# Turning the first experts' rows two blocks ahead, and loading their weights one round sooner

## The chip, the cores and the metric

The kernel runs on one core of a Trainium2 chip. The metric is the device time of one execution in microseconds, as the median of several runs. All engines of the core have their own instruction queues: PE (TensorE), DVE (VectorE), ACT (ScalarE), POOL (GpSimd) and SP (SyncE, which here only issues transfers). An engine works through its queue in order and waits on semaphores that other engines or transfers raise.

## The reference

Two layers follow one another on 32 sequences of 56 tokens with 256 features. What matters here is the first mixture of experts: 16 experts of width 176, six chosen for each token.

```python
x = x + _L0_xattn_ref(_layernorm(x), ctx_2048, ...)   # a scan over 1500 context rows, only its mean is used
x = x + _L0_ffn_ref(_layernorm(x), ...)               # 16 experts, width 176, top 6
x = x + _L1_xattn_ref(_layernorm(x), ctx_2048, mask)  # masked attention over the context
x = x + _L1_ffn_ref(_layernorm(x), ...)               # 2 experts, width 1024, top 1

# _L0_ffn_ref, for the tokens h
scores = softmax(h @ gate_w.T)
topk_w, topk_idx = top_k(scores, 6)
for e in range(16):
    out = silu(h @ w_gate[e].T) * (h @ w_up[e].T) @ w_down[e].T
    y = y + cw[:, e:e+1] * out                        # cw: the chosen scores, zero elsewhere
```

## The kernel before

The kernel has four stages in time. The context stage reads the whole context (32 loads of 1.5 MB into a ring of five slots), makes the first layer's sum, normalizes the tokens, and sorts the tokens by expert. The first experts' stage runs over 95 blocks of 128 sorted rows. Then come the second layer's attention and its two experts.

**The context stage** goes in rounds. A round `p` (two sequences, 112 tokens) calls the steps of a list in an order written out by hand, each for its own `p` plus an offset. Tokens are written as normalized rows: `second_norm` makes the tile `xn` on ACT (L563), out of a pool of four buffers, so that the tile of one `p` takes the buffer of `p - 4`; `away` (L569) sends it from SP to `xn0` in HBM. In round `p` it is `away(p - 1)` that is issued. `count_in` reads a ring slot on PE (L339) and issues the load of the context five sequences on (L155, SP).

**The first experts' weights** come on the same SP queue. `load_w0_up` issues four transfers of 1.4 MB (L206: 2,048 pieces of 704 bytes each) after round 12, the last of `away(11)`. The down weights are 26 small transfers (L222) of 8 to 88 partitions; `some_pieces(n)` issues the next `n` of them, here six after round 13, six after round 14, and the other 14 in the tail, after `away(b)` and `away(c)`.

**The tail** finishes the last three rounds' tokens, called a, b and c in the code (13, 14 and 15). Its order is also written by hand. It ends with `idx`, the table of the row numbers of all 95 blocks, and `wgt`, their weights (L902, L903). `busy(n)` puts n matmuls on PE whose result nobody reads. The sort of a token group needs `tokens_in` (ACT, L655), `ones_at` or `low_ones` (DVE, L666), `more_ones` (POOL, L674) and `last_ones` (ACT, L692 and L695) before `sorted_low` and `sorted_high` (PE, L702).

**The first experts' stage** is `expert_blocks` with one unit a block. `rows_of` gathers a block's 128 rows from `xn0` into a tile `xb` (POOL, L1092, eight buffers, seven gathers ahead). It reads all of `xn0`, so the first gather waits for every `away` to have landed, and for `idx`. `turned_rows` transposes `xb` on PE and copies it to `xT` on ACT (L191, L193, three buffers). In iteration `t`, PE does: gate and up matmuls of block t (L933), transposes of the hidden rows of block t-1 (L951), transposes of the rows of block t+1 (L191), down matmuls of block t-2 (L960). ACT does: the activation of block t (L939), the copy of `xT` of block t+1 (L193), the copy of the result of block t-2 (L1100). DVE multiplies and copies (L945, L953). Beside these, `side(t)` puts in small work of the next stage; among it up to one or two gathers of finished rows an iteration on POOL (L1007), from iteration 20 on.

Of the kernel before, what the change touches and what calls it, by code (L numbers as in the profile page):

```python
# [22 lines left out]
NP = B // 2  # L23
# [37 lines left out]
def xattn_ffn_kernel(  # L61
# [149 lines left out]
    def w0_down_pieces():  # L211

        half = E0 // 2
        for e in range(half):
            for c in range(2):
                r = 0
                while r < H0:
                    f = e * F0 + c * H0 + r
                    n = min(H0 - r, P - f % P)
                    o = 2 * KD * F0 + c * D  # L220
                    k = f // P
                    yield lambda r=r, n=n, e=e, o=o, f=f, k=k: nc.sync.dma_start(  # L222
                        out=w0_sb[r : r + n, e :: half, o : o + D],
                        in_=wd0[f % P : f % P + n, k :: half * F0 // P, :][:, 0:2, :],
                    )
                    r += n

    with tc.tile_pool(name="p1", bufs=1) as p1, tc.tile_pool(name="p3", bufs=3) as p3, tc.tile_pool(
# [185 lines left out]
        def first_stats(o):  # L414
            for p in range(o, o + 4):
                V.bn_stats(out=st[:, p, :], in_=xr[:, p, :])
                V.bn_aggr(out=mva[:, p, :], in_=st[:, p, :])
            inverse_root(rsa[:, o : o + 4], mva[:, o : o + 4, 1])

        def first_bias(o):  # L420
            q = slice(o, o + 4)
            V.scalar_tensor_tensor(nba[:, q], mva[:, q, 0], -1.0, rsa[:, q], ALU.mult, ALU.mult)
# [145 lines left out]
        def away(p):  # L568
            nc.sync.dma_start(out=xn0[p * P : (p + 1) * P, :], in_=pend[p]["xn"])  # L569
# [23 lines left out]
        def scores_out(p):  # L593
            A.copy(lgs[p % 2][:, 0:E0], pend[p]["lp"][:, 0:E0])
# [58 lines left out]
        def tokens_in(p):  # L653
            v = vals[:, p % 2]
            A.activation(v[:, :, 0, :], v[:, :, 0, :], AF.Copy, scale=ids[:, p : p + 1])  # L655

        def hots(p, h):
            t = pend[p].setdefault("hots", {})
            if h not in t:
                t[h] = ohp.tile([P, NE, P], F32, tag="oh", name="oh")  # L660
            return t[h]

        def ones_at(p, h, n=NE):

            o = NE * h
            V.tensor_tensor(  # L666
                hots(p, h)[:, 0:n], iota.unsqueeze(1).to_broadcast([P, n, P]),
                pend[p]["off"][:, o : o + n].unsqueeze(2).to_broadcast([P, n, P]), ALU.is_equal,
            )
# [9 lines left out]
        def busy(n, w=512):  # L679

            for _ in range(n):
                d = psa.tile([P, 512], F32, tag="acc", name="d")
                PE.matmul(
                    d[:, 0:w], lhsT=ident, rhs=ones[:, 0:1].to_broadcast([P, w]),
                    start=True, stop=True,
                )

        def last_ones(p, h, n):

            t, off = hots(p, h)[:, n:NE], pend[p]["off"]  # L690
            for i in range(n, NE):
                A.activation(  # L692
                    t[:, i - n], iota, AF.Abs, bias=off[:, NE * h + i : NE * h + i + 1], scale=-1.0
                )
            A.activation(t, t, AF.Relu, bias=ones[:, 0:1], scale=-1.0)  # L695
# [19 lines left out]
        def low_ones(p):  # L715
            ones_at(p, 0)
# [16 lines left out]
        pieces = list(w0_down_pieces())  # L733


        def some_pieces(n):
            for _ in range(n):
                if pieces:
                    pieces.pop(0)()
# [22 lines left out]
        for p in range(last):  # L762
            for step, d in steps if p == last - 1 else steps + ends:
                if 0 <= p + d < NP:
                    step(p + d)
            if p < 3:
                first_stats(4 * p + 4)
                first_bias(4 * p + 4)
            if p == NP - 4:
                load_w0_up()  # L770
            if p > NP - 4:
                some_pieces(6)


        at_ = slots[B % NRING].rearrange("p j d -> p (j d)")[0:1, CW - 2 * E0 * NLP :]
        G.memset(at_, 0.0)
        at_ = at_.rearrange("p (e o l) -> p e o l", e=E0, o=2)
        a, b, c = last - 2, last - 1, last
        scores_out(a)
        sum_in_columns(c)  # L780
# [24 lines left out]
        away(b)  # L805
        second_norm(c)
        away(c)
        some_pieces(len(pieces))
        places(a)
        turned(b)  # L810
        more_high_ones(a)
# [22 lines left out]
        PE.matmul(tot[:, 0:E0], lhsT=ones, rhs=chosen[:, b % 2], start=False, stop=True)  # L834
        more_high_ones(b)
        ranks(c)
        busy(2)
        real = p2.tile([P, NL, E0], F32, name="real")
        V.tensor_tensor(
            real, tot[:, 0:E0].unsqueeze(1).to_broadcast([P, NL, E0]), lev, ALU.is_gt  # L840
# [20 lines left out]
        for k in range(4):  # L861
# [3 lines left out]
                rhs=ones[0:1, 0:1], start=True, stop=True,  # L865
            )
        low_ones(c)
        last_ones(c, 1, 6)
        tokens_in(c)
        ones_at(c, 1, 6)  # L870
        sorted_low(c)
        blk = p2.tile([P, 4], F32, name="blk")
# [41 lines left out]
    def expert_blocks(nb, nq, f, w, ei, wk, ptr, pgu, pht, py, rows_of, done, ahead, wgt=None, side=None, xT0=None):  # L914

        fp = f // nq
        h = fp // 2
        doff = 2 * KD * fp
        piece = doff + 2 * D
        units = [(i, u) for i in range(nb) for u in range(nq)]  # L920
        xT, at, hs, hT, y = {}, {}, {}, {}, {}

        def expert_at(i):
            at[i] = PE.value_load(
                ei[0:1, i : i + 1], min_val=0, max_val=w.shape[1] - nq * piece
            )

        def gate_up(i, u):
            if u == 0 and i not in at:
                expert_at(i)  # L930
            gu = pgu.tile([P, 512], F32, tag="gu", name="gu")
            for k in range(KD):
                PE.matmul(  # L933
                    gu[:, 0 : 2 * fp], lhsT=xT[i][:, k, :],
                    rhs=w[:, bass.ds(at[i] + (u * piece + k * 2 * fp), 2 * fp)],
                    start=(k == 0), stop=(k == KD - 1),
                )
            sg = wk.tile([P, fp], F32, tag="sg", name="sg")
            A.activation(sg, gu[:, 0:fp], AF.Silu)  # L939
            hs[i, u] = wk.tile([P, fp], F32, tag="hs", name="hs")  # L940
            up = gu[:, fp : 2 * fp]
            if wgt is None:
                V.tensor_tensor(hs[i, u], sg, up, ALU.mult)  # L943
            else:
                V.scalar_tensor_tensor(hs[i, u], sg, wgt[:, i : i + 1], up, ALU.mult, ALU.mult)  # L945

        def turn(i, u):
            tp = pht.tile([P, 512], F32, tag="ht", name="tp")
            a = hs.pop((i, u))
            for c in range(2):  # L950
                PE.transpose(tp[0:h, c * P : (c + 1) * P], a[:, c * h : (c + 1) * h], ident)  # L951
            hT[i, u] = wk.tile([h, 2 * P], F32, tag="hT", name="hT")
            V.tensor_copy(hT[i, u], tp[0:h, 0 : 2 * P])  # L953

        def down(i, u):
            if u == 0:
                y[i] = py.tile([P, 512], F32, tag="y", name="y")
            a = hT.pop((i, u))
            for c in range(2):
                PE.matmul(  # L960
                    y[i][:, 0:D], lhsT=a[:, c * P : (c + 1) * P],
                    rhs=w[0:h, bass.ds(at[i] + (u * piece + doff + c * D), D)],
                    start=(u == 0 and c == 0), stop=(u == nq - 1 and c == 1),
                )
            if u == nq - 1:
                done(i, y.pop(i))

        xb = {i: rows_of(i) for i in range(min(ahead, nb))}
        if not xT0:
            unread(ptr, "tr", 512, 512, 512, 256)  # L970
            expert_at(0)
        xT[0] = xT0 or turned_rows(wk, ptr, "tr", xb[0])
        xb.pop(0)
        if side:
            side(-1)
        for t in range(len(units) + 2):
            if t < len(units):
                gate_up(*units[t])
            if 0 <= t - 1 < len(units):
                turn(*units[t - 1])  # L980
            if t < len(units) and units[t][1] == nq // 2 and units[t][0] + 1 < nb:
                i = units[t][0] + 1
                if i + ahead - 1 < nb:
                    xb[i + ahead - 1] = rows_of(i + ahead - 1)
                xT[i] = turned_rows(wk, ptr, "tr", xb.pop(i))
            if t >= 2:
                down(*units[t - 2])
            if side:
                side(t)
# [89 lines left out]
    with tc.manual_schedule(  # L1079
# [10 lines left out]
        def rows_of(i):  # L1090
            xb = xbp.tile([P, D], F32, tag="xb", name="xb")
            G.indirect_dma_start(  # L1092
                out=xb, out_offset=None, in_=xn0,
                in_offset=bass.IndirectOffsetOnAxis(ap=idx[:, i : i + 1], axis=0),
            )
            return xb
# [170 lines left out]
    with tc.manual_schedule(  # L1267
# [214 lines left out]
        for p in range(NP + 1):  # L1482
# [17 lines left out]
            if p < NP:  # L1500
                nb = highest(sps)
# [159 lines left out]
    with tc.tile_pool(name="g", bufs=2) as gp, tc.tile_pool(name="g1", bufs=1) as g1, tc.tile_pool(  # L1661
# [12 lines left out]
        for p in range(NP):  # L1674
# [41 lines left out]
            nb = small.tile([P, 3], F32, tag="nb", name="nb")  # L1716
# [119 lines left out]
```

## Time and profile before

| | us |
|---|---|
| median of 3 runs | 703.46 |
| lowest, highest | 700.73, 703.96 |
| the profiled execution's own time | 743.97 |
| its span | 742.3 |
| PE busy | 674.1 (91%) |
| DVE, ACT, POOL busy | 386.9, 258.5, 318.0 |
| HBM traffic | 136.63 MB, 184 GB/s over the span |

The profiled execution took 40.5 us more than the median of the runs. Its durations are those of the instructions and waits in that execution, so a sum of them belongs to 743.97 us first. PE's busy time counts matmuls whose ends are modelled. The page gives shares over the whole span, while the change touches two places: the end of the context stage (about 130 to 186 us) and the first experts' stage (about 186 to 470 us).

### The profile page before, as it was taken

What the parts mean: (1) busy time and instruction counts of PE and PEld (TensorE: products, weight loads), DVE (VectorE), ACT (ScalarE), POOL (GpSimd) and SP (SyncE); (2) the same over time, 40 slices, a digit from 0 to 9 for tenths busy, and PEclk for the clock granted to TensorE, in tenths of its full rate; (3) what the DMA queues carried; (4) which work ended last, traced back from release to release, by engine and by line L of the source; (5) the groups of instructions that cost most, each with busy time, mean ns of one, the idle gap of its engine ahead of it and who ended that gap; (6) DMA issues with size and microseconds to landing.
All of it is one profiled execution on the core that took longest, in us unless ns stands there. A gap on an engine that the chain in (4) does not pass through costs nothing.

```text
span 742.3 us, 13524 instructions
## 1 busy us (share of the span) xinstructions
PE 674.1 (91%) x4111; PEld 434.3 (59%) x4111; DVE 386.9 (52%) x1310; ACT 258.5 (35%) x772; POOL 318.0 (43%) x416
## 2 busy tenths in 40 slices
PE   7789999998799888898898888999897999999997
PEld 3345565654577565566676655566554666666564
DVE  5548888885256344343353436568787332323232
ACT  0224555542244333333343332476552111111110
POOL 3104454544543664667656655558423302122111
PEclk7858999998899999999999999999999999999999
DMA  8999999995489874444444444595941201010100
GB/s 272 337 406 404 410 411 411 384 287 147 133 260 282 292 217 149 121 128 128 135 128 136 128 124 119 149 329 79 333 143 62 88 15 33 32 38 28 35 30 18
DMA packets 71273, 136.63 MB, mean 184 GB/s; under 512 B 8026, under 2 KB 43772, under 8 KB 71196
## 3 DMA queue, kind: packets, MB, share of 16 engines
q1 hardware_dynamic: 56042, 100.31, 38.6%
q0 software_dynamic: 14096, 34.52, 17.1%
q10 hardware_dynamic: 1058, 0.86, 0.4%
q8 instruction: 38, 0.62, 0.4%
q14 instruction: 39, 0.32, 0.1%
HBM read 109.54 MB, written 26.77 MB: 184 GB/s over the span
## 4 chain that ended last, share of the span: by engine, by line
PE 65%; DVE 4%; issue 2%; ACT 2%; SPq 1%; DMA 1%; POOL 0%; another core or an unknown queue 0%; POOLq 0%; ACTq 0%; DVEq 0%
PE gu L933 30%; PE y L960 19%; PE tp L951 4%; PE tp L191 3%; PE tp L1064 3%; PE sp L1294 2%; PE op L1329 2%; SPq L222 1%; ACT xT L193 1%; PE tp L1053 1%; PE tp L1321 1%; PE sp L1288 1%; DMA w_sb<-in_wd 1%; DMA xs<-pay,to 0%; POOL oh L674 0%
## 5 line engine op out<-in xcount | busy, mean ns | idle before, releaser
L933 PE MATMUL gu<-w_sb,xT 128*128 x380 | 134.3, 476 | 29.4 <-ACT xT L193 19.8
L939 ACT ACTIVATE sg<-gu 128x176 f32<-128x176 f32 (+1 forms) x155 | 53.3, 344 | 247.0 <-PE gu L933 213.0
L1092 POOL DMA_INDIRECT xb<-xn,idx x95 | 94.0, 989 | 95.5 <-PE tp L191 43.3
L945 DVE SCALAR_TENSOR_TENSOR hs<-sg,wgt,gu 128x176 f32<-128x176 f32 x95 | 37.7, 397 | 154.5 <-ACT sg L939 129.2
L933 PE MATMUL gu<-ring,xT 128*128 x240 | 113.8, 597 | 0.0
L933 PEld LDWEIGHTS gu<-w_sb,xT 128*128 128x128 f32 x380 | 69.9, 192 | 65.4 <-ACT xT L193 27.8
L960 PE MATMUL y<-w_sb,hT 88*128 x380 | 98.6, 382 | 1.6 <-ACT yb L1100 1.6
L1007 POOL DMA_INDIRECT g<-ys,early x78 | 74.6, 956 | 35.3 <-issue 20.4
L943 DVE TENSOR_TENSOR hs<-sg,gu 128x256 f32<-128x256 f32 x60 | 25.3, 421 | 112.2 <-ACT sg L939 108.3
L951 PEld LDWEIGHTS tp<-ident,hs 128*88 128x88 f32 (+1 forms) x310 | 40.3, 130 | 58.7 <-issue 47.9
L960 PEld LDWEIGHTS y<-w_sb,hT 88*128 88x128 f32 x380 | 65.0, 191 | 7.4 <-ACT yb L1100 2.0
L1580 POOL DMA_INDIRECT out<-ob,ti x15 | 14.8, 990 | 126.9 <-DVE ob L1577 126.6
L674 POOL TENSOR_SCALAR oh<-iota,off 128x128 f32<-128x128 f32 x60 | 42.5, 722 | 59.0 <-PE owned L702 39.8
L953 DVE COPY hT<-tp 88x256 f32<-88x256 f32 (+1 forms) x155 | 64.4, 415 | 4.8 <-PE y L960 4.0
L933 PEld LDWEIGHTS gu<-ring,xT 128*128 128x128 f32 x240 | 45.6, 192 | 33.3 <-issue 30.5
L339 PE MATMUL acc<-ring,cz 128*32 128x256 f32 x768 | 57.0, 438 | 5.8 <-DMA ring<-in_cx 5.4
L960 PE MATMUL y<-ring,hT 128*128 x240 | 61.7, 380 | 0.0
L951 PE MATMUL tp<-ident,hs 128*88 128x128 f32 (+1 forms) x310 | 59.5, 274 | 0.0
L193 ACT COPY xT<-tp 128x256 f32<-128x256 f32 x110 | 41.0, 373 | 41.9 <-PE y L960 21.3
L1100 ACT COPY yb<-y 128x256 f32<-128x256 f32 x95 | 35.7, 376 | 47.0 <-PE y L960 27.2
L191 PE MATMUL tp<-ident,xb 128*128 128x128 f32 x220 | 42.5, 275 | 0.9 <-DMA xb<-xn,idx 0.9
L960 PEld LDWEIGHTS y<-ring,hT 128*128 128x128 f32 x240 | 41.0, 190 | 3.3
(315 smaller groups left out, 967.5 us busy)
## 6 DMA issues: line engine op xcount, KB each, us to landing
ring<-in_cx SPq DMA_DIRECT2D x32, 1536.0 KB
ys<-yb SPq DMA_DIRECT2D x95, 128.0 KB
ring<-in_cx SPq DMA_DIRECT2D x16, 384.0 KB
extra<-in_cx SPq DMA_DIRECT2D x16, 384.0 KB
xs<-zrow SPq DMA_DIRECT2D x5, 771.0 KB
w_sb<-in_wg SPq DMA_DIRECT2D x2, 1408.0 KB
w_sb<-in_wu SPq DMA_DIRECT2D x2, 1408.0 KB
xn<-xn SPq DMA_DIRECT2D x16, 128.0 KB
```

The costliest lines, as they stand in the source:

```text
L191: PE.transpose(tp[:, k * P : (k + 1) * P], xn[:, k * P : (k + 1) * P], ident)
L193: A.copy(xT.rearrange("p k c -> p (k c)"), tp[:, 0 : KD * P])
L339: PE.matmul(acc[Q * g : Q * g + Q, 0:D], lhsT=cz[:, j, 1 - h : 1 - h + Q], rhs=c[:, j, :], start=(h == 0 and m == 0), stop=(h == 1 and m = ...
L674: G.tensor_scalar(hots(p, h)[:, i, :], iota, pend[p]["off"][:, NE * h + i : NE * h + i + 1], None, ALU.is_equal,)
L933: PE.matmul(gu[:, 0 : 2 * fp], lhsT=xT[i][:, k, :], rhs=w[:, bass.ds(at[i] + (u * piece + k * 2 * fp), 2 * fp)], start=(k == 0), stop=(k = ...
L939: A.activation(sg, gu[:, 0:fp], AF.Silu)
L945: V.scalar_tensor_tensor(hs[i, u], sg, wgt[:, i : i + 1], up, ALU.mult, ALU.mult)
L951: PE.transpose(tp[0:h, c * P : (c + 1) * P], a[:, c * h : (c + 1) * h], ident)
L953: V.tensor_copy(hT[i, u], tp[0:h, 0 : 2 * P])
L960: PE.matmul(y[i][:, 0:D], lhsT=a[:, c * P : (c + 1) * P], rhs=w[0:h, bass.ds(at[i] + (u * piece + doff + c * D), D)], start=(u == 0 and c ...
L1007: G.indirect_dma_start(out=g, out_offset=None, in_=ys0[0 : n * P, :], in_offset=bass.IndirectOffsetOnAxis(ap=at[:, p, k : k + 1], axis=0),)
L1092: G.indirect_dma_start(out=xb, out_offset=None, in_=xn0, in_offset=bass.IndirectOffsetOnAxis(ap=idx[:, i : i + 1], axis=0),)
```

## The change

Four edits. The rows of a first-experts block are transposed and copied two blocks before they are used, in place of one (block 1 and block 2 still one ahead; in iteration 2 both block 3 and block 4). The gate and up weights' four transfers are issued after round 11, in place of round 12, and so stand on SP's queue ahead of `away(11)`. The down weights are issued eight after each of the rounds 12, 13 and 14, and the other two at the start of the tail, so that all 26 stand ahead of `away(b)` and `away(c)`, in place of 12. In the tail, one of two unread matmuls is left out of `busy`, and `tokens_in(c)` goes ahead of `last_ones(c)` on ACT. The second experts' blocks, which also use `expert_blocks`, keep their order (`nq > 1`).

```diff
-            if p == NP - 4:
+            if p == NP - 5:
                 load_w0_up()
-            if p > NP - 4:
-                some_pieces(6)
+            if p > NP - 5:
+                some_pieces(8)
...
+        some_pieces(len(pieces))
         a, b, c = last - 2, last - 1, last
         scores_out(a)
...
         away(b)
         second_norm(c)
         away(c)
-        some_pieces(len(pieces))
         places(a)
...
         ranks(c)
-        busy(2)
+        busy(1)
...
         low_ones(c)
+        tokens_in(c)
         last_ones(c, 1, 6)
-        tokens_in(c)
         ones_at(c, 1, 6)
...
+        def turned_at(i, u):
+            if nq > 1:
+                return [j for j in (i + 1,) if u == nq // 2 and j < nb]
+            return [j for j in ((i + 1,) if i < 2 else (3, 4) if i == 2 else (i + 2,)) if j < nb]
...
-            if t < len(units) and units[t][1] == nq // 2 and units[t][0] + 1 < nb:
-                i = units[t][0] + 1
+            for i in turned_at(*units[t]) if t < len(units) else ():
                 if i + ahead - 1 < nb:
                     xb[i + ahead - 1] = rows_of(i + ahead - 1)
                 xT[i] = turned_rows(wk, ptr, "tr", xb.pop(i))
```

## The prediction

> **What bounds the kernel now.** First the times by stage, in four windows cut at the first and the last experts' matmuls (columns: PE, weight loads, DVE, ACT, POOL busy, granted clock, DMA share, GB/s).
>
> ```profile
> 0.00:186.30 186.30, 164.56 (x1694) 95.16 (x1694) 134.19 (x459) 76.96 (x263) 72.64 (x129) 0.87 0.96 346
> 186.30:470.00 283.70, 251.63 (x1162) 180.66 (x1162) 125.91 (x411) 99.80 (x289) 164.11 (x171) 0.98 0.54 164
> ...
> 570.00:742.30 172.30, 165.86 (x612) 101.37 (x612) 52.87 (x161) 27.04 (x71) 31.21 (x35) 0.99 0.12 35
> ```
>
> The context stage moves 346 GB/s at a DMA share of 0.96: transfers bound it. The experts' stages belong to PE. Then SP's timeline (start, length, transfers), because the change moves only transfers there:
>
> ```profile
> 131.70 0.37 SPq L155 DMA_DIRECT2D ring<-in_cx  x1
> 134.89 0.34 SPq L569 DMA_DIRECT2D xn<-xn  x1
> 135.32 10.62 SPq L206 DMA_DIRECT2D w_sb<-in_wg  x2
> 146.00 9.35 SPq L206 DMA_DIRECT2D w_sb<-in_wu  x2
> 155.44 3.66 SPq L569 DMA_DIRECT2D xn<-xn  x1
> 159.14 4.88 SPq L222 DMA_DIRECT2D w_sb<-in_wd  x6
> 164.44 0.37 SPq L569 DMA_DIRECT2D xn<-xn  x1
> 165.06 4.82 SPq L222 DMA_DIRECT2D w_sb<-in_wd  x6
> 169.98 1.77 SPq L569 DMA_DIRECT2D xn<-xn  x2
> 171.80 10.74 SPq L222 DMA_DIRECT2D w_sb<-in_wd  x14
> ```
>
> SP is busy without a break from 135 to 182.5. An `away` costs 0.34 to 0.45 when nothing holds it; 3.66 at 155.44 means that the queue was full. Last, the start of the first experts, in PE's timeline and POOL's:
>
> ```profile
> 184.07 0.41 PE L191 MATMUL tp<-ident,xb 128*128 128x128 f32 x2 [0.89 <-DMA xb<-xn,idx]
> 186.37 1.56 PE L933 MATMUL gu<-w_sb,xT 128*128 x4 [1.89 <-DMA w_sb<-in_wd]
> ```
>
> ```profile
> 180.53 1.19 POOL L1092 DMA_INDIRECT xb<-xn,idx  x1 [9.82 <-ACT wgt L903]
> ```
>
> Rows are gathered from 180.53, after the table (POOL's wait ends at 179.65), and the first gate matmul starts at 186.37, when the last down weights have landed. The first `xT` was ready at 184.94 (ACT's copy, 184.57 + 0.37): the weights cost 1.4 us. And PE's waits from 186 to 470 (total, times, longest):
>
> ```profile
> PE gu L933 <- ACT xT L193: 19.8, 19, 2.1
> PE gu L933 <- issue: 6.4, 9, 1.5
> ...
> PE gu L933 <- DMA w_sb<-in_wd: 1.9, 1, 1.9
> ```
>
> **Two blocks ahead.** No operation is added: 95 pairs of transposes and 95 copies, each an iteration sooner, and POOL's gathers likewise; POOL runs eight blocks ahead, limited by its buffers. In an undisturbed iteration (gate matmuls at 206.28 and 208.77) PE has no gap: 1.19 gate and up, 0.22 + 0.22 transposes, 0.86 down make 2.49. `xT` is ready at 206.04 and its weight load starts at 206.10, so the old order is just in time, and the new one gains nothing there. It gains where ACT was late. From the first gate matmul at 186.37 to the last at 467.73 are 281.4 us; 94 x 2.49 = 234.1; so 47.3 us are surplus, of which 19.8 wait for `xT`. But this execution is 743.97 and the runs' median 703.46: 40.5 us are not in the runs. The last stage goes at PE's pace (60 units of 2.80, without gaps), the context stage at 410 GB/s, the attention in rounds of 4.96; none has room for 40 us, the first experts' surplus does. If all 40.5 sit there, 6.8 are left in a run, and the share of `xT` waits (19.8/47.3 = 0.42) makes 2.9. If half sit there, 27 are left and 11.3 go. The low end is 0. I take half of 2.9, so -1.4: of the 6.8 about 2.6 are the eight iterations of 2.82 with context transposes between, which are PE's own work, and blocks 1 and 2 keep the old order. In the profile itself up to 26 (19.8 + 6.4) could go; I expect 13.
>
> **Gate and up weights sooner.** On SP they follow the last context load, at 132.1 in place of 135.3: 3.2 us sooner, not a round of 7.5, because SP reaches that place only then. Do they land sooner? The DMA share in 2 us slices is 1.02 to 1.06 until 144 and 1.06 to 1.21 until 162: always full. The semaphores' updates in the trace show the last context landed at 141.3 to 145.8 and the four weights at 150.8, 155.5, 159.3 and 164.4; SP finishes issuing each when the one two before it has landed. So they are paced by the drain and land as before. The Trainium skill's page DMA: Bandwidth & Descriptors, under Rules for kernel authors, says the opposite in general: issue early, compute, wait late, and the cost overlaps. By that rule the whole SP queue is 3.2 us sooner; by these rows, by nothing. I follow the rows, and keep the rule as a rival.
>
> What the move does do: `away(11)`, at 134.89 before and landed at 146.1, now stands behind the weights, where `away(12)` stood, which landed at 165.0; without one `away` ahead of it, 164.7. Its buffer is the one that `second_norm(c)` writes (15 - 4 = 11). That ran at 161.48; it will wait until 164.7, 3.2 us, and behind it on ACT stand both `turned_out`, then the scores of b and c; PE's `turned(c)` and both gates, DVE's `best(b)` and all behind it wait for those. No spare work fills this, so the table, 179.65 before, moves by all 3.2.
>
> **Small edits in the tail.** `busy(2)` took 3.76 us (167.81 to 171.5), so one less frees PE 1.9 sooner; DVE's `low_ones(c)` had waited 0.43 for the buffer that PE's sort of b then frees. `tokens_in(c)` moves from 174.72 to about 172.3, and `sorted_low(c)` (175.27, after a gap of 0.63) with it. The table comes sooner by 0.43 at the least and 1.0 at the most; I take 0.7: 179.65 + 3.2 - 0.7 = 182.15.
>
> **Down weights ahead of the last rows.** The 26 pieces take 4.88 + 4.82 + 10.74 = 20.4 us of SP in either order. In the new one, SP is through the held `away(11)` at 159.1; 20.4 of pieces, three `away` at about 0.45 and gaps put `away(c)`'s start at 181.15. In the profile `away(c)` landed 2.57 after its start (170.53 to 173.10), so now at 183.7. Before, the landing at 173.10 had 6.5 us to spare against the table; now it comes last, 1.55 after the table. The first gather may go at 183.7 in place of 179.65: 4.05 later, and `xT` at 189.0. The weights have landed by then, so their 1.4 are gone, and the first gate matmul starts at 189.05, against 186.37: **+2.7**.
>
> **Sum.** +2.7 - 1.4 = +1.3. On the profiled time: 743.97 + 2.7 - 13 = 733.7. On the median, with the stalls left in a run: 703.46 + 1.3 = **704.8**. A measurement of this kernel can tell about 0.5%, 3.5 us, from no change (its three runs spread over 3.2).
>
> **Rivals.** A: as summed, 704.8, its own range 702 to 708.
>
> B, slower: the wait of `second_norm(c)` lets PE go cold. PE has then some 3.2 us of nothing between `turned(b)` and `turned(c)`, with `busy` halved later. The trace shows the granted clock at 0.50 in 154 to 156 and 168 to 172; 32 sort matmuls took 1.08 at full clock and 1.94 at half. The skill's page TensorE: Matmul & The Clock Gate, Part 1, gives an idle window of about 3.4 us for the halving; 3.2 is just under it, while the rows fell to half in 168 to 172 with PE shown busy. By the rule nothing is added; by the rows: 0.86 for the last sort, about 1.3 for the table's own matmuls (1.92 at full), about 1.4 for transposes, gates and ranks (2.8): 3.6 in all. The table is then at 185.75, and passes the landing of `away(c)` as the last one once more than 1.55 is added. The first gate matmul moves by 4.7; with no gain in the blocks: 708.2.
>
> C, faster: the waits for `xT` are in the runs also, at the high end of 11.3: 703.46 + 2.7 - 11.3 = 694.9, or 698 at two thirds. For it: 19 separate waits, and `xT` ready only 0.06 us ahead of its weight load. Against it: the 40.5 us have to sit somewhere, and in the stalled iterations (gate matmul at 263.45, 0.98 late) ACT and POOL are released within 0.02 us (262.97, 262.98) and signals of DVE and of a transfer arrive in the same 0.06, as if all signals were late, not ACT.
>
> D: the change does not do what it seems to on SP, the whole queue being 3.2 sooner. Then `second_norm(c)` does not wait, `away(c)` lands at 180.5, the gate matmul starts at 185.9 (-0.5), and with -1.4 the time is 701.6.
>
> **How the numbers follow.** A 0.45, B 0.25, C 0.17, D 0.13. Faster by over 0.5%: C and a little of A and D, 0.19. Slower: B nearly whole and 0.08 of A, 0.31. Same: the rest, 0.50. Range for 8 in 10: cutting about half of C's chance below and a third of B's above, 698 to 709.5.
>
> **What would show it.** SP's last `away` ends at about 181.6 and no down-weight transfer follows it; on ACT the second `second_norm` of the tail starts 3 us after the first, not 0.5; POOL's first gather starts at about 184.6, released by a transfer of `xn` rather than by `wgt`; the first gate matmul at about 189, released by `xT`. PE's wait for `xT` falls from 19.8 to under 5 and the surplus over 2.49 an iteration falls in the profile. Wrong, if SP finishes the four weights well before 155 (then D), if the first gather is released by the table (then B or D), or if the runs fall by more than 3.5 us (then C).

## The result, and the profile of the changed kernel

| | before | changed |
|---|---|---|
| median of 8 runs, us | 703.0 (700.73 to 703.96) | 706.82 (704.22 to 709.34) |
| ratio | 1 | 1.0065, 95% interval 1.0041 to 1.0088 |
| profiled execution, us (span) | 743.97 (742.3) | 707.09 (705.4) |

The change costs 3.8 us. A ratio leaves out runs over 1.5% above the fastest of the same kernel; that bears only on the second chip below, where it leaves out 5 of 67 runs of before and between none and six of the others'. The two profiled executions can't be subtracted: the one of before has some 38 us in the first experts' stage that its runs don't have (the first experiment comes back to that). The place where the change works, the end of the context stage, can be compared step by step.

The windows view of the changed kernel, cut as before at the first and the last gate matmul of the first experts (columns: PE, weight loads, DVE, ACT, POOL busy, granted clock, DMA share, GB/s):

```profile
0.00:190.70 190.70, 161.05 (x1692) 94.97 (x1692) 135.43 (x459) 75.49 (x262) 70.32 (x128) 0.87 0.95 339
190.70:434.00 243.30, 238.32 (x1152) 178.93 (x1153) 123.83 (x406) 103.29 (x289) 161.22 (x171) 1.00 0.64 190
...
530.00:705.40 175.40, 167.54 (x612) 102.08 (x612) 54.16 (x166) 26.89 (x71) 31.11 (x35) 0.99 0.11 35
```

The context stage is 4.4 us longer than in the profile of before (190.70 against 186.30). From the first to the last gate matmul of the experts it is 243.0 against 281.4 (the windows are cut a little later than the last one, by 0.3 and 2.3), and PE is busy for 238.3 of it: next to nothing is left to gain there.

SP's timeline (start, length, transfers):

```profile
131.06 15.55 SPq L206 DMA_DIRECT2D w_sb<-in_wg  x2
146.66 9.04 SPq L206 DMA_DIRECT2D w_sb<-in_wu  x2
155.80 3.72 SPq L569 DMA_DIRECT2D xn<-xn  x1
159.56 7.71 SPq L222 DMA_DIRECT2D w_sb<-in_wd  x8
167.38 0.46 SPq L569 DMA_DIRECT2D xn<-xn  x1
167.89 6.26 SPq L222 DMA_DIRECT2D w_sb<-in_wd  x8
174.25 0.44 SPq L569 DMA_DIRECT2D xn<-xn  x1
174.74 7.66 SPq L222 DMA_DIRECT2D w_sb<-in_wd  x10
182.51 0.91 SPq L569 DMA_DIRECT2D xn<-xn  x2
```

The gate and up weights begin at 131.06, 4.3 sooner than in the profile of before, and SP is through with them at 155.70, where it was at 155.34. The sooner start went into a longer issue (15.55 for the first two, against 10.62). By the updates of their semaphores in the trace the four landed at 151.30, 155.81, 159.64 and 165.76, and in the profile of before at 150.77, 155.51, 159.30 and 164.37: no sooner. `away(11)` stands behind them, and no down weights stand behind the last two `away`, which landed at 185.47 and 185.79. Among the first eight down weights SP stood still once, for the landing of the fourth of these loads (from SP's waits between 155 and 185; total, times, longest):

```profile
SPq L222 <- DMA w_sb<-in_wu: 1.3, 1, 1.3
```

ACT's timeline, the last two `second_norm`, and PE's at the same place:

```profile
159.17 0.58 ACT L563 ACTIVATE xn<-xr,mv 128x256 f32<-128x256 f32 x1
166.05 0.60 ACT L563 ACTIVATE xn<-xr,mv 128x256 f32<-128x256 f32 x1 [6.30 <-DMA xn<-xn]
```

```profile
159.80 0.44 PE L574 MATMUL tp<-ident,xn 128*128 128x128 f32 x2 [1.15 <-ACT xn L563]
166.70 0.69 PE L574 MATMUL tp<-ident,xn 128*128 128x128 f32 x2 [6.46 <-ACT xn L563]
```

`second_norm(c)` waits 6.30 us for `away(11)`, which landed at 165.96, and PE has nothing from 160.24 to 166.70. `wgt`, the end of the table, is ready at 184.96 (179.84 before).

POOL's first gather, and PE's start of the first experts:

```profile
186.68 1.19 POOL L1096 DMA_INDIRECT xb<-xn,idx  x1 [10.42 <-DMA xn<-xn]
```

```profile
189.81 0.41 PE L191 MATMUL tp<-ident,xb 128*128 128x128 f32 x2 [1.52 <-DMA xb<-xn,idx]
190.74 1.45 PE L933 MATMUL gu<-w_sb,xT 128*128 x4 [0.52 <-ACT xT L193]
```

The gather is released by a transfer of `xn`, that is by the last rows, and the first gate matmul by `xT`, no longer by the weights. It starts at 190.74, 4.4 after the 186.37 of before.

### The profile page after: what moved, and what is told of

Same layout as the page of the kernel before. It is cut to its first block, busy times and chain, and to the rows that moved or that the text cites. A ratio compares the mean times of both kernels' runs of the same rounds, so it can differ in the third digit from the quotient of the medians.

```text
span 705.4 us, 13597 instructions
## 1 busy us (share of the span) xinstructions
PE 657.3 (93%) x4109; PEld 433.3 (61%) x4109; DVE 387.4 (55%) x1310; ACT 261.0 (37%) x772; POOL 315.4 (45%) x416
## 4 chain that ended last, share of the span: by engine, by line
PE 77%; DMA 10%; DVE 6%; ACT 3%; SPq 2%; issue 1%; POOL 0%; POOLq 0%; DVEq 0%; ACTq 0%
PE gu L933 30%; PE y L960 19%; DMA ring<-in_cx 7%; PE acc L339 5%; PE tp L951 5%; PE tp L191 3%; PE tp L1068 2%; PE sp L1298 2%; PE op L1333 2%; DMA xn<-xn 2%; PE sT L520 1%; PE bp L531 1%; SPq L250 1%; SPq L222 1%; PE lp L587 1%
## 5 line engine op out<-in xcount | busy, mean ns | idle before, releaser
L933 PE MATMUL gu<-w_sb,xT 128*128 x380 | 128.8, 460 | 2.8 <-ACT xT L193 1.4
L1096 POOL DMA_INDIRECT xb<-xn,idx x95 | 91.5, 964 | 60.5 <-PE tp L191 31.8
L951 PEld LDWEIGHTS tp<-ident,hs 128*88 128x88 f32 (+1 forms) x310 | 40.0, 130 | 59.3 <-issue 47.0
L951 PE MATMUL tp<-ident,hs 128*88 128x128 f32 (+1 forms) x310 | 59.5, 274 | 0.5 <-DVE mv L1026 0.5
```

Source lines behind the costliest of these rows:

```text
L933: PE.matmul(gu[:, 0 : 2 * fp], lhsT=xT[i][:, k, :], rhs=w[:, bass.ds(at[i] + (u * piece + k * 2 * fp), 2 * fp)], start=(k == 0), stop=(k = ...
L1096: G.indirect_dma_start(out=xb, out_offset=None, in_=xn0, in_offset=bass.IndirectOffsetOnAxis(ap=idx[:, i : i + 1], axis=0),)
```

## The experiments

The kernels ran in three sets, each on one chip beside the kernel before: before took 703.77 us (31 runs) in the first set (the first four experiments), 747.74 (67 runs, 742.1 to 756.0) on another chip in the second (the next four), and 703.17 (36 runs) in the third (the last four). Ratios are to before on the same chip.

Where all the kernels agree is set out first, as the experiments refer to it (us from the start of each profiled execution; "table" is the end of `wgt`, "rows" the landing of the last `away`; the last gate matmul is that of the last block, and the experts' stage runs from the first to it; all come from the traces, each from one execution):

| kernel | table | rows | first gather | first gate matmul | experts' stage | last gate matmul | time against before |
|---|---|---|---|---|---|---|---|
| before, profile on record | 179.84 | 173.10 | 180.53 | 186.37 | 281.4 | 467.73 | - |
| before again | 182.41 | 173.38 | 183.11 | 187.94 | 243.2 | 431.13 | (one run) |
| turning alone | 180.09 | 173.18 | 180.78 | 185.89 | 244.5 | 430.36 | 1.0004 |
| gate and up sooner alone | 186.95 | 173.38 | 187.64 | 191.60 | 243.2 | 434.82 | 1.0044 |
| down weights first alone | 178.12 | 183.97 | 184.87 | 189.15 | 245.7 | 434.85 | 1.0055 |
| changed | 184.96 | 185.79 | 186.68 | 190.74 | 243.0 | 433.74 | 1.0065 |
| changed again | 186.56 | 184.83 | 187.25 | 191.23 | 243.1 | 434.31 | 1.0070 |
| changed, five `xn` | 177.03 | 184.59 | 185.50 | 189.72 | 245.3 | 435.00 | 1.0077 |
| turning and tail | 177.93 | 173.44 | 178.62 | 186.15 | 244.4 | 430.56 | 1.0012 |
| same, down in two after the rows | 180.20 | 165.65 | 180.89 | 187.18 | 244.4 | 431.56 | 1.0009 |
| *second chip:* changed, five `xn` | 180.66 | 185.15 | 186.05 | 190.04 | 275.3 | 465.37 | 1.0010 |
| gate and up sooner, five `xn` | 182.81 | 175.17 | 183.51 | 188.15 | 286.5 | 474.60 | 0.9986 |
| tail alone | 182.04 | 172.88 | 182.74 | 187.93 | 281.9 | 469.86 | 0.9955 |
| turning, tail, down in two | 179.65 | 184.09 | 184.99 | 189.16 | 278.3 | 467.47 | 0.9968 |

In all fourteen rows the first gather starts 0.69 to 0.70 after the table, or 0.89 to 0.91 after the last rows, whichever is later. The table and the rows lie beside each other, and only the later one opens the gather.

What a late start costs in the end is read at the last gate matmul. On the 703 us chips it is at 430.4 to 431.1 (mean 430.7) in the three profiles with SP's old order, and at 433.7 to 435.0 in the five with one or both SP edits. The stage has not the same length everywhere on these chips: it is 243.0 to 243.2 in four profiles, and 244.4 to 245.7 in the other five. The reason lies in its first matmuls. The first four gate and up matmuls take 1.45 us where PE had stood at most 1.6 us for the first gathered rows and nothing more for the weights (six of the fourteen profiles), and 2.71 or 2.72 where it had stood 5.0 to 8.2 us for the rows (four of them). A late release of the gathers with the table long ready therefore costs twice: PE starts late, and it starts at half the clock (shown under "down weights ahead of the last rows" and in the run with five `xn`).

### The kernel before, once more

> The kernel before, unchanged, for a second trace. Theory S (the 40 us of stalls in the first experts' stage belong to that one execution): the span is near 702 us, PE's waits for xT before the gate matmuls are under 5 us in total and the first to last gate matmul take 238 to 245 us. Rival C (the waits for xT are the normal state and the new order removed them): the span is again over 730 us and the waits for xT again about 20 us.

Measured: 702.68 us, span 701.0. Windows view of this profile, its experts' stage, and PE's waits in it (total, times, longest):

```profile
187.90:431.20 243.30, 238.32 (x1152) 178.49 (x1153) 123.51 (x406) 103.33 (x288) 159.96 (x171) 1.00 0.63 189
```

```profile
PE gu L933 <- ACT xT L193: 1.4, 3, 0.5
```

Of the 41.3 us between the two spans, 38.2 lie between the first and the last gate matmul of the experts (243.2 against 281.4). The 19.8 us of waits for `xT` are 1.4 in an execution of 703. There is next to nothing for the second block of lead to remove.

### Turning two ahead, alone

```diff
-            if t < len(units) and units[t][1] == nq // 2 and units[t][0] + 1 < nb:
-                i = units[t][0] + 1
+            for i in turned_at(*units[t]) if t < len(units) else ():
```

> Only the turning two blocks ahead. Theory S: within 1 us of the kernel before (703.0), at best -1.4; nothing before the first gate matmul moves. Rival C: 5 us or more faster. Rival T (the new order costs something in the blocks): 1 us or more slower, and part of the loss of the whole change is here.

Measured: 704.37 us, ratio 1.0004 (0.9981 to 1.0026). PE's wait for `xT` is 0.9. The stage takes 244.5 us, 1.3 more than in the profile of before again; here its first gate matmuls had waited for the down weights and ran in part at half the clock (1.83 us for four). Where they did not, the stage takes 243.0 and 243.1 with turning (the changed kernel's two profiles) and 243.2 twice without (before again; gate and up sooner alone). On this chip the edit is worth nothing that can be measured.

### Gate and up weights sooner, alone

```diff
-            if p == NP - 4:
+            if p == NP - 5:
                 load_w0_up()
```

> Only the four gate and up transfers issued one round sooner, the down pieces as before. Theory W (the rows of round 11 stand behind 5.8 MB of weights and hold the buffer that the last second_norm writes): the last second_norm starts 4 to 6 us later, the table of rows comes at 183 to 186 in place of 179.65, the first gate matmul at 188 to 191; 2 to 4.5 us slower. Rival O (only the order of the last rows behind the down pieces matters): within 0.5 us of before.

Measured: 706.40 us, ratio 1.0044 (1.0027 to 1.0062), so about 3 us. ACT's and POOL's timeline:

```profile
158.72 0.58 ACT L563 ACTIVATE xn<-xr,mv 128x256 f32<-128x256 f32 x1
164.98 0.60 ACT L563 ACTIVATE xn<-xr,mv 128x256 f32<-128x256 f32 x1 [5.68 <-DMA xn<-xn]
```

```profile
187.64 1.19 POOL L1092 DMA_INDIRECT xb<-xn,idx  x1 [12.43 <-DMA ring<-in_cx]
```

The last rows are there at 173.38, so the table alone opens the gather, at 186.95 + 0.69. (The releaser that the row names is the signal that came last by the profile; the semaphores of `xn` show that no rows were due.) The wait of `second_norm(c)` alone costs these 3 us.

### Down weights ahead of the last rows, alone

```diff
-                some_pieces(6)
+                some_pieces(8)
...
         at_ = at_.rearrange("p (e o l) -> p e o l", e=E0, o=2)
+        some_pieces(len(pieces))
         a, b, c = last - 2, last - 1, last
...
         away(c)
-        some_pieces(len(pieces))
```

> Only the down pieces ahead of the last two row transfers (eight after rounds 13 and 14, the other ten at the start of the tail), the gate and up weights as before. Theory O (the last rows land behind all pieces, and the first gather waits for them): the table stays at 179 to 180, the last rows land at 183.5 to 186, the first gate matmul is at 188.5 to 191; 2 to 4.5 us slower. Rival W alone: within 0.5 us of before, or 1.4 faster because the down weights land sooner.

Measured: 707.85 us, ratio 1.0055 (1.0028 to 1.0081). SP's timeline, POOL's and PE's:

```profile
166.61 13.99 SPq L222 DMA_DIRECT2D w_sb<-in_wd  x18
180.70 0.91 SPq L569 DMA_DIRECT2D xn<-xn  x2
```

```profile
184.87 1.19 POOL L1092 DMA_INDIRECT xb<-xn,idx  x1 [16.31 <-DMA xn<-xn]
```

```profile
187.98 0.66 PE L191 MATMUL tp<-ident,xb 128*128 128x128 f32 x2 [6.52 <-DMA xb<-xn,idx]
189.15 2.72 PE L933 MATMUL gu<-w_sb,xT 128*128 x4 [0.52 <-ACT xT L193]
```

The table is ready at 178.12 and the rows land at 183.97: the gather waits 6 us with the table at hand. PE stands 6.5 us for the gathered rows, and then the granted clock is 0.50 from 189.15 to 193.4. So this kernel's first gate matmul comes 2.5 us sooner than that of the edit before, but the last one at the same time (434.85 and 434.82).

This edit, too, costs about 4 us by itself. The two SP edits would make 7.0 if they added up (0.44% and 0.55% of 703.77 are 3.1 and 3.9, with intervals of 1.9 to 4.4 and 2.0 to 5.7); the whole change costs 3.8 (2.9 to 6.2). The traces say the same: against the mean of 430.7 the last gate matmul is 4.1 and 4.2 later with one edit, and 3.1 and 3.6 in the two profiles of the whole change.

### The changed kernel with a fifth `xn` buffer

```diff
-        name="xn", bufs=4
+        name="xn", bufs=5
```

> The changed kernel with five xn buffers in place of four: the last second_norm no longer waits for the rows of round 11; nothing else moves. Theory P (the two waits lie beside each other, and either alone costs nearly the whole): the last second_norm follows the one before it at once, the table is ready at 177 to 181, but the last rows still land at 184 to 186 and the first gather still starts at about 185 to 187; the time stays within 1.5 us of the changed kernel (706.8), at least 2 us over before. Rival Q (the wait of second_norm is the cost and the late rows are hidden by it alone): within 1 us of before.

Measured: 749.18 us, ratio 1.0010 (0.9981 to 1.0040), on the second chip. The two `second_norm` run one after the other (159.54, 160.03), the table is ready at 180.66, and POOL waits on for the rows:

```profile
186.05 1.19 POOL L1096 DMA_INDIRECT xb<-xn,idx  x1 [16.51 <-DMA xn<-xn]
```

So without the wait the gather is held as long by the rows. The time is level with before nonetheless. This chip's executions have the stalls of the profile on record, and the stage is shorter in its two profiles with turning (275.3, 278.3) than in its two without (286.5, 281.9); turning alone was not run on this chip, so that it makes up for the SP edits here is likely and not shown. The ratio therefore can't say alone what the SP edits cost; the third set repeats the run beside the changed kernel.

### Gate and up weights sooner, with a fifth `xn` buffer

```diff
-            if p == NP - 4:
+            if p == NP - 5:
                 load_w0_up()
...
-        name="xn", bufs=4
+        name="xn", bufs=5
```

> The gate and up weights one round sooner, with five xn buffers, the down pieces as before. Theory P with the drain (starting sooner gains nothing because the transfers are paced by the 16 engines, which are full): SP ends the four issues at 155 to 156 as before, the first gate matmul is where the kernel before has it, and the time is within 1 us of before. Rival R (starting sooner shifts the queue by 3 us): SP ends the four issues at 152 to 153, the down weights land 3 us sooner, 1 to 2 us faster than before.

Measured: 747.26 us, ratio 0.9986 (0.9959 to 1.0013). SP's timeline:

```profile
133.99 13.04 SPq L206 DMA_DIRECT2D w_sb<-in_wg  x2
147.09 9.27 SPq L206 DMA_DIRECT2D w_sb<-in_wu  x2
```

This is the test of the rule that the prediction took from the Trainium skill's page DMA: Bandwidth & Descriptors, Rules for kernel authors (issue early, wait late): with the harm taken away, the sooner load is left alone. The page says only that the fixed setup cost of a transfer overlaps; that the whole queue would be sooner was the prediction's reading of it. The load begins 3.5 us sooner than in the run that follows, on the same chip (137.45), and SP ends it at 156.36, where it ends at 155.88 there; the last of the four landed at 164.88 and 164.92. The time is that of before. Behind transfers that already fill the queue, the sooner start buys nothing that can be measured here (this pair was run on the second chip alone).

### The order in the tail, alone

```diff
-        busy(2)
+        busy(1)
...
-        last_ones(c, 1, 6)
         tokens_in(c)
+        last_ones(c, 1, 6)
```

> Only one unread matmul less and tokens_in ahead of last_ones in the tail. Theory: the table comes 0.4 to 1.0 us sooner after the last second_norm than in the kernel before at the same granted clock; the first gate matmul then waits for the down weights (185 to 186.5), so the time is within 0.7 us of before. Rival (the matmul kept the clock up): the granted clock in 170 to 180 is lower, the table 1 to 3 us later, 1 us or more slower.

Measured: 746.04 us, ratio 0.9955 (0.9929 to 0.9980). From `second_norm(c)` to the table it takes 19.49 us, and 20.19 in the run above at the same granted clock (0.74 and 0.75): the 0.7 expected of the edit. The ratio stands for 3.4 us, more than a table 0.7 sooner can give, but the means over all 22 and 67 runs differ by only 1.3 (95% interval -0.8 to 3.3). That is no gain clear of noise, and the third set (turning and tail, 1.0012) shows none either. PE's waits in the experts' stage of this profile, and of the changed kernel with five `xn` buffers, which turns two ahead (total, times, longest):

```profile
PE gu L933 <- ACT xT L193: 23.7, 20, 3.7
```

```profile
PE tp L951 <- DVE hs L945: 7.7, 6, 2.0
PE tp L951 <- issue: 4.1, 2, 2.2
...
PE gu L933 <- ACT xT L193: 2.3, 5, 0.7
```

On this chip the waits for `xT` exist. They are 21 us less in the profile with the second block of lead, but the stage is only 6.6 shorter (275.3 against 281.9). PE comes to wait in the next step instead, the hidden rows' transposes (L951), and its gate and up matmuls themselves took 487 ns in the mean against 478. `xT` was the one late signal that the profile named, not the only one that was late.

### Turning and tail, with the down weights in two transfers

SP's order is that of before, and the down weights come from an array laid out for it, so that two transfers of 88 partitions take the place of the 26. Both are issued after round 13.

```diff
-        for e in range(half):
-            for c in range(2):
-                ...
+        for e in (0, half):
+            yield lambda e=e: nc.sync.dma_start(
+                out=w0_sb[0:H0, e : e + half, 2 * KD * F0 : W0], in_=wd0[:, e : e + half, :]
+            )
```

> The kernel before with the down weights laid out so that two transfers of 88 partitions take the place of the 26 pieces (no piece left in the tail), and with the turning two ahead and the two tail edits. The same is computed. Theory: SP is through with all weights by 166 to 170, the last rows land before 177, the first gate matmul waits for the table alone and starts 5.3 us after it (184 to 187): 0.5 to 2.5 us faster than before. Rival (the down weights were hidden anyway, and two transfers on 11 of the 16 engines hold back the last rows): the first gather starts later than the table, slower than before.

Measured: 745.68 us, ratio 0.9968 (0.9940 to 0.9997). SP's timeline:

```profile
159.20 2.70 SPq L215 DMA_DIRECT2D w_sb<-in_wd  x2
162.00 8.57 SPq L560 DMA_DIRECT2D xn<-xn  x3
```

The two loads are issued in 2.7 us where 26 took 20, but they landed at 174.79 and 183.16, and the three `away` behind them at 183.43, 183.75 and 184.09. The first gather waits until 184.99 with the table ready at 179.65. Fewer transfers did not bring the rows in sooner, since the rows still stood behind the same weights.

### The changed kernel again, and with five `xn` buffers, on one chip

> The changed kernel once more, on the chip of the three runs that follow. Theory (the two moves on SP lie beside each other: the gathers open when the later of table and last rows is there, 185 to 186 in the trace): where the kernel before takes about 703 us, +3 to +5 us (ratio 1.004 to 1.008), first gate matmul at about 190.5; where it takes about 748, turning ahead gives 5 us back in the first experts' stage, so 0.998 to 1.003. Rival (the moves add up): last rows and table more than 3 us apart, first gate matmul at 193 or later, 1.009 or more.

> The changed kernel with five xn buffers, so that the second_norm of the last block waits for no transfer. Theory (last rows behind all the down weights hold the gathers by themselves): table at about 180, last rows still at about 185, first gate matmul within 1 us of the changed kernel's, time within 1.5 us of it. Rival (the wait of second_norm is what costs): 3 to 4 us less than the changed kernel, level with the kernel before where that takes 703.

Measured: 708.16 us, ratio 1.0070 (1.0048 to 1.0092), and 708.65, ratio 1.0077 (1.0052 to 1.0102). POOL's timeline of the first and of the second, then PE's waits of the second:

```profile
187.25 1.19 POOL L1096 DMA_INDIRECT xb<-xn,idx  x1 [11.99 <-DMA ring<-in_cx]
```

```profile
185.50 1.19 POOL L1096 DMA_INDIRECT xb<-xn,idx  x1 [17.15 <-DMA xn<-xn]
```

```profile
PE tp L191 <- DMA xb<-xn,idx: 8.2, 1, 8.2
```

With the fifth buffer the table is ready at 177.03, 9.5 us sooner than in the run beside it, and the first gate matmul comes only 1.5 sooner (189.72 against 191.23): PE stands 8.2 us in one wait for the first gathered rows. In the medians not even the 1.5 can be seen, and the traces show why. PE's first gate and up matmuls, and the windows view of the 4.3 us from there, of the first:

```profile
191.23 1.45 PE L933 MATMUL gu<-w_sb,xT 128*128 x4 [0.52 <-ACT xT L193]
```

```profile
191.23:195.50 4.27, 3.55 (x14) 2.11 (x14) 0.70 (x2) 2.37 (x5) 3.34 (x4) 1.00 0.36 100
```

and of the second (the granted clock is the third number from the end):

```profile
189.72 2.72 PE L933 MATMUL gu<-w_sb,xT 128*128 x4 [0.52 <-ACT xT L193]
```

```profile
189.72:194.00 4.28, 3.82 (x7) 2.14 (x8) 0.40 (x1) 1.94 (x3) 3.37 (x4) 0.50 0.39 111
```

After the long wait PE begins the experts at half the clock. The last gate matmul is at 435.00, 0.7 later than in the run beside it. So the wait of `second_norm(c)` is not by itself what the change costs; without it, the late rows and the slow start cost as much. In the first of the two, the table (186.56) was later than the rows (184.83); in the profile shown above it was the other way round.

### Turning and tail, with SP's order of before

> Two parts of the change together, turning two ahead and the order in the tail, with SP's order as before. Theory (both SP moves cost, the other two parts are worth 0 and 0.7): gathers released by the table, at 180 to 182; 0 to 1.5 us less than the kernel before where that takes 703 (0.998 to 1.000), 3 to 7 us less where it takes 748 (0.991 to 0.996). Rival (the parts' gain is spent at the end of the stage): 1.000 in either case.

Measured: 703.89 us, ratio 1.0012 (0.9990 to 1.0035): no difference. PE's waits:

```profile
PE gu L933 <- DMA w_sb<-in_wd: 3.0, 1, 3.0
```

The table was ready at 177.93 and the first `xT` at 183.62, and the first gate matmul still started at 186.15, when the last down weights had landed (186.01). In SP's old order these weights are a floor, at 184.7 to 186.0 in the profiles of the 703 us chips: a sooner table ends in this wait. With the whole SP change taken back and the rest kept, the cost is gone, so it is the SP edits' cost.

### The same, with the down weights in two transfers behind the last rows

The edit is that of the run with two transfers, and these are issued after `away(c)`, none in the rounds before.

```diff
             if p == NP - 4:
                 load_w0_up()
-            if p > NP - 4:
-                some_pieces(6)
```

> As the run before, and the 26 down-weight transfers are two (88 partitions each, from a layout made for it in the inputs), issued behind the last rows. Theory: rows land by 167, the two loads by 183 (8 to 9 us each where they stood ahead of the rows), before the first xT at 185: gathers released by the table at 180 to 182, first gate matmul by xT; 0 to 1.5 us less than turning and tail alone. Rival (two slow loads land after xT, or hold the context loads behind them): first gate matmul released by in_wd, 1 to 3 us more than turning and tail alone.

Measured: 704.27 us, ratio 1.0009 (0.9981 to 1.0037). SP's timeline and PE's:

```profile
156.09 6.83 SPq L560 DMA_DIRECT2D xn<-xn  x4
162.97 1.11 SPq L215 DMA_DIRECT2D w_sb<-in_wd  x2
```

```profile
186.26 0.41 PE L191 MATMUL tp<-ident,xb 128*128 128x128 f32 x2 [2.72 <-DMA xb<-xn,idx]
187.18 2.26 PE L922 MATMUL gu<-w_sb,xT 128*128 x4 [0.52 <-ACT xT L193]
```

The rows land at 165.65, the table opens the gather, and the weights' wait is gone. But the two loads landed only at 175.24 and 185.10, and the first gather, begun at 180.89, was complete at 186.17, after them; in the run of turning alone PE had its rows at 184.24 from a gather begun at 180.78. The start is bound by the same transfers once more, as far as this one profile shows, and the time is that of before. No version found is faster than the kernel before where that takes 703 us.

## Why the prediction was right, and where it was off

The forecast was 704.8 with a range of 698 to 709.5; measured 706.82. It lies in the likeliest case's own range (702 to 708), but past the 0.5% that the text set as what can be told from no change, so it falls under "slower", to which the text gave 0.31. Step by step:

- **Gate and up weights sooner, +0: right.** SP was through with the four at 155.70 (155.34 before), they landed no sooner, and the weights sooner alone, without the wait behind them, measure 0.9986. Rival D, the whole queue sooner, fell with it, and with it the reading that a load issued early is a queue done early.
- **The wait of `second_norm(c)`: right in kind, too small.** `away(11)` landed at 165.96 where 164.7 was expected; the wait itself is 6.30, since in this execution the norm of b came 1.8 sooner. From there to the table 18.91 us passed, where the step had 17.66 (18.36 of before less 0.7). So the table moved by 5.1 and not by 2.5.
- **The tail, -0.7: about right as a size, as far as pairs of single profiles tell, and without effect.** It measures 0.7 and, between the changed kernel with five `xn` (18.27) and turning alone (19.27) at clocks of 0.72 and 0.73, 1.0; at 0.81 it is nothing (18.36 before, 18.40 turning and tail). It is hidden by the down weights in the old SP order and by the last rows in the new.
- **The last rows: right in kind, 2.1 late.** They were put at 183.7 and came at 185.79. The 26 pieces took 21.6 us of SP and not 20.4. The issues themselves took no longer; SP stood 1.3 us among the first eight, before the seventh, which shares its semaphore with the fourth gate and up load and waited for that to land (165.76; the row of SP's wait stands with the timeline above). A further 0.4 came from the held `away(11)`, the rest from the gaps between and the landing (2.7 after the start). "Comes last, 1.55 after the table" holds as 0.83 in this profile and is reversed by 1.7 in the other.
- **The first gate matmul, +2.7: under-sized.** It measured +4.4 against the profile on record. Three other profiles with SP's old order on the 703 us chips have it at 187.94, 185.89 and 186.15, in the mean 186.7; against these the changed kernel's two profiles (190.74, 191.23) are 4.1 and 4.6 later. Of this, about 1 us is not a cost: two of those three began the experts partly at half the clock, after waits for the down weights, and at the last gate matmul the change is 3.1 and 3.6 later.
- **Turning two ahead, -1.4: wrong, 0.** The inference that the 40.5 us of the profile are not in the runs was right and placed rightly. But then 2.9 us of `xT` waits were carried over as a share, and half of them taken; they are 1.4, three times at most 0.5, and the changed kernel has the same 1.4. For the profile itself -13 was expected; on the chip with the stalls the stage was 6.6 shorter in one pair of profiles. Rival C fell (its sum at two thirds is 698.6, not 698).
- **Rival B, 708.2,** had the start at +4.7, near what was measured. The idle time of PE that it weighed as 3.2 us was 6.46. PE's granted clock between `second_norm(c)` and the table was 0.67, 0.53 and 0.61 in the three profiles with the wait, and 0.68 to 0.91 in those of kernels on the 703 us chips without it; the tail took 18.91, 21.52 and 21.97 against 18.2 to 21.0. So a part of B is in the traces. How large a part stays open: the 0.68 was measured without the wait, and the kernel with five `xn` buffers, which has neither the wait nor the late table, costs the same. That kernel too pays in clock, but at another place, at the start of the experts, which no case of the prediction had.

The forecast was +1.3 and the medians differ by 3.8, so the sum was short by 2.5: 1.4 of turning that is not there, 0.4 to 0.9 of the start as it is left at the last gate matmul, and a rest that is within what the runs can tell. What the prediction had right, and what carries the result, is that the two SP edits put the last rows at the end of the queue, so that they and the table are due at the same time.

## What to carry to other kernels

When a change moves small stores behind large loads on one queue, ask of each store who reads what it wrote and who reuses its buffer: here one `away` held the buffer of the next tile and two others held all gathers, and each alone cost 3 to 4 us. Two such costs that lie beside each other are not added, and mending one shows little until the other is mended too. And a wait is not over when it ends, if PE had nothing to do in it: after 5 to 8 us its first matmuls took nearly twice as long. A profile slower than the runs must be repeated before its waits are taken as gains: the largest wait in it was 19.8 us, and in an execution at the median 1.4.

## What the runs showed of the hardware

- The same program takes 703 us on two chips and 748 on another. Of the 43.7 us between two spans (before again, 701.0; tail alone, 744.7), 38.7 lie in the first experts' stage (243.2 against 281.9). PE is busy 13.3 us longer in it (238.3 against 251.6; the granted clock is 1.00 against 0.97, by an estimate from these some 7 of the 13), and idle 25.4 longer. What makes signals late there was not found. The profile on record (742.3, stage 281.4) looks like one of the second chip's; on which chip it was taken is not known.
- PE that had stood 5.0 to 8.2 us began its work at half the clock in all four profiles that have such a wait. Where it stood 6.52 and 8.18 us (down weights first alone; five `xn` again), the granted clock is 0.50 in the 4.3 us from the first gate matmul, and the first four take 2.72; where it stood 1.52 and 0.40 (the changed kernel's two profiles), it is 1.00 and they take 1.45.
- The last part of the context stage, nearly the same instructions in each, takes 18.2 to 22.0 us from one execution to another at granted clocks from 0.91 to 0.53; the two go together only loosely (18.27 at 0.72, 21.04 at 0.68, the latter with one unread matmul more). In the windows view of the kernels with the highest and the lowest clock (down weights in two after the rows; changed again):

```profile
161.99:180.20 18.21, 14.62 (x165) 10.23 (x165) 14.41 (x45) 6.39 (x21) 7.91 (x9) 0.91 0.77 176
```

```profile
165.04:186.56 21.52, 20.30 (x163) 15.46 (x163) 12.92 (x39) 6.29 (x20) 4.87 (x5) 0.53 0.51 151
```

- Two transfers of 1.4 MB to 88 partitions took about 10 us each (landed at 175.24 and 185.10, issued at 163), while the core's DMA share read 0.71 to 0.80 and 151 to 180 GB/s; the context loads ran at 410 GB/s. In the trace each of the two raises its semaphore eleven times at its landing, a 128-partition load sixteen times, and 11/16 is 0.69. That they are few instructions did not make them fast.
